# A two-layer graph kernel: five blocks of layer 0 one step later, the last rows' x in a tile of its own, and the next pair turned inside the current pair's products

## The chip, the cores and the metric

The kernel runs on one core of one Trainium2 chip. The metric is the device time of one execution in microseconds (us). The time before is the median of 13 runs, 1067.2 us. The core's engines work at the same time, each through its own queue in order: PE (TensorE, matrix products, with PEld for its weight loads), DVE (VectorE), ACT (ScalarE), POOL (GpSimd, here mostly indirect DMAs that gather or scatter rows) and SP (SyncE, which issues plain DMAs).

## The reference

`x` has 2708 rows of 1024 numbers, `adj` is a sparse 2708 x 2708 matrix of zeros and ones, and everything is float32.

```python
# layer 0
q = x @ W_q.T + b_q;  k = x @ W_k.T + b_k;  v = x @ W_v.T + b_v
z = (q @ k.T) / sqrt(1024) * adj
attn = softmax(where(z == 0, -10000, z), axis=1)
x = layernorm(x + relu(attn @ v))
# layer 1
x = layernorm(x + adj @ (x @ weight) + bias)
```

## The kernel before

**Sparse form.** The kernel lists the few neighbours of each row and sorts the rows by their number. The sorted rows form 22 blocks of 128; block `b` has `SLOTS[b]` neighbours for each row (block 0 has 15, blocks 18 to 20 have one, block 21 holds rows without neighbours). A block's part in layer 0 is: gather a row of `y` for each of its rows and the `x` rows of its neighbours (POOL, line 349), score them (DVE, line 813), softmax, add up the weighted neighbours into a tile `r` (DVE, line 870), turn `r` with 8 PE transposes per row block (line 716) and an ACT copy out of PSUM (line 717), and multiply by `W_v` ("project"). The 32 busiest rows, the "hub", are dealt over the whole tile and joined with block 0 (lines 947 to 967).

**The y stage.** `y` is x times a product of the key and query weights. `y_block(b)` runs 16 matmuls of 128x512 for 128 rows of x (line 319), two DVE adds out of PSUM into the tile `yo` (line 323), 8 column sums on ACT (line 332), the load of a later block's transposed x into one of three tiles `xt`, and a store of `yo`. Block 21 holds only 20 rows of x and goes another way (line 305). After it `xbT`, the mean of x, is ready, which the blocks with few neighbours need.

**The list of steps in layer 0.** `steps` is written out by hand. ("y", b) is a block of the y stage. ("v", b) projects one block alone (line 739); it is followed, at the next step, by `finish0`, whose two DVE bias adds (line 906) take the products out of PSUM. ("p", pair) projects two blocks at once. Before each step `run_job` is called as long as a written credit lasts; each call gathers and scores a piece of one block. Jobs in `late_jobs` start when the y stage is over. The names `got`, `turned` and `done0` keep which blocks are added up, turned and done. At most three tiles `r` (`RB`) are held at a time.

**Pairs.** For two blocks the product with a 1024x1024 matrix is taken in seven half products instead of eight (one level of Winograd's scheme). `turn_pair` turns both blocks and forms four sums `S` of the turned halves on DVE (lines 988 to 991) in one buffer, `s_all`. `differences` are three or four differences of weight quarters. `pair_products` issues the seven half products, each 4 matmuls of 128x512 (line 999), into PSUM banks `pa`, `pb`, `pc`, with DVE adds between them (line 1011). Its first two products, `a11 * w11` and `a12 * w21`, need only the turned block, the others need `S` or the second block. Layer 1 works the same way in `units` of one or two blocks: `sum_rows` adds up gathered rows of layer 0's output (line 1241), `gather_x1` prepares x plus bias (line 1251 and a gather), `turn1` turns, `work1` multiplies, `finish1` normalizes and scatters. The adds marked `URGENT` go ahead in DVE's order.

**What sets the order.** The order in which the Python code issues instructions, with a scheduler's priorities, sets each engine's queue. So where the code issues a turning decides what stands in front of it on PE, and whatever stands behind a DVE or POOL instruction that waits, waits too.

Of the kernel before, what the change touches and what calls it, by code (L numbers as in the profile page):

```python
# [80 lines left out]
def sparse_part(ctx, tc, x, xT, adj, wqT, wkT, wvT, bq, bk, bv, w1, b1, out):  # L81
# [29 lines left out]
    with es:  # L111
# [158 lines left out]
        xts = []  # L270

        def load_x():
            b = len(xts)
            if b == NB:
                return
            r0, n = b * P, rows[b]
            xt = xa.tile([P, DC, P], F32, name="xt", bufs=3)
            if n < P:
                nc.gpsimd.memset(xt, 0.0)
            nc.sync.dma_start(out=xt[:, :, :n], in_=xT[:, r0:r0 + n].rearrange("(c p) n -> p c n", p=P))  # L280
            xts.append(xt)
# [48 lines left out]
        def column_sums(b, behind=None):  # L330
            for c in range(DC):
                put = nc.scalar.activation(junka, xts[b][:, c, :], AF.Copy, accum_out=xs[:, c, b:b + 1])  # L332
                if behind is not None and c % 2 == 0:
                    follow(put, behind[c // 2])
# [642 lines left out]
        def turn_pair(flips, pool):  # L977

            A = []
            for k, flip_to in enumerate(flips):  # L980
                rT = (pool if k else wp).tile([P, DC, P], F32, name="rT", bufs=2)
                A.append(flip_to(rT))
            if len(flips) == 1:
                return A, None
            (a11, a12), (a21, a22) = [(a[:, :DC // 2], a[:, DC // 2:]) for a in A]
# [5 lines left out]
            halves_turned.append(nc.vector.tensor_sub(S[3], a12, S[1]))  # L991
            return A, S

# [18 lines left out]

        def pair_products(A, S, w, ts, base, to, whole, first_alone=False):

# [8 lines left out]
            half_products(pb, a12, w21)  # L1023
            whole(0, 0, pb, to[0][0])
            if first_alone:
                half_products(pc, S[0], t1, stop=False)
# [25 lines left out]

        def project_pair(pair, A, S):
# [6 lines left out]
            pair_products(A, S, wv_q, wv_t, [bias, bias], [halves_of(t) for t in ts], whole, pair == pairs[-1])  # L1060
            return ts

        def finish_pair(pair, ts):
            for k, (b, t) in enumerate(zip(pair, ts)):
# [9 lines left out]
                else:  # L1074
# [13 lines left out]
        jobs, late_jobs = jobs + late_jobs, len(late_jobs)  # L1088
        steps = [("y", 8), ("y", 9), ("y", 10), ("y", 11), ("y", 12), ("v", 6), ("y", 13), ("v", 5), ("y", 14), ("v", 4), ("y", 15), ("v", 3),
                 ("y", 16), ("v", 2), ("y", 17), ("y", 18), ("y", 19), ("y", 20), ("y", 21)]  # L1090
        steps += [("v", b) for b in [1, 0] + last] + [("p", pair) for pair in pairs]
# [16 lines left out]
        def turn0(b):  # L1108
# [4 lines left out]
            return flip_shares([got["hub"], got[0]]) if b == 0 else flip(got[b])  # L1113

        credit = -STEP
        turned, done0 = {}, set(last)
        pending = None
        left_y = NB - FAMILY
        for i, (kind, b) in enumerate(steps):
# [29 lines left out]
            for k, c in steps[i:i + 2]:  # L1149
                if k != "y" and c not in turned and not (left_y and k == "p"):  # L1150
                    turned[c] = turn0(c) if k == "v" else turn_pair([lambda rT, r=got[b_]: flip(r, rT) for b_ in c], xb_pools[0])
                    done0.update(blocks_of((k, c)))
            if kind == "y":
# [11 lines left out]
            elif kind == "v":  # L1165
                xr = gather_x(x, b)
                pending = finish0, b, (project_mean if b in last else project)(turned[b], wv_q), xr
            else:
                for b_ in b:
                    pair_x[b_] = gather_x(x, b_)  # L1170
                pending = finish_pair, b, project_pair(b, *turned[b])
        w1_q = quarters_of("w1")
# [97 lines left out]

        def work1(unit, A, S, xrs):

# [13 lines left out]
            if S is None:  # L1286
                (a11, a12), x0 = halves_of_turned(A[0]), xs_[0]
                pa, pb = bank(), bank()
                half_products(pa, a11, w11, stop=False)
                add(x0[1], pa, x0[1])  # L1290
                half_products(pb, a11, t1, stop=False)
                half_products(pb, a12, w22, start=False)
# [3 lines left out]
            else:  # L1296
                pair_products(A, S, w1_q, w1_t, xs_, xs_, whole, unit == units[-1])
            return ts, sums
# [3 lines left out]
        got1[1] = [sum_rows(b, k) for k, b in enumerate(units[1])]  # L1302
        turned1[0] = turn1(units[0], got1.pop(0))
        follow(nc.vector.tensor_sub(t1, t1, w11), firsts[0], same=True)
        nc.vector.tensor_sub(t2, w22, t1)
# [3 lines left out]
        for i, unit in enumerate(units):  # L1309
            for p in pending:  # L1310
                finish1(*p)
            if i + 1 < len(units):
                turned1[i + 1] = turn1(units[i + 1], got1.pop(i + 1))
                xrs[i + 1] = [gather_x1(b, k) for k, b in enumerate(units[i + 1])]
            if i == 0:
                got1[2] = [sum_rows(b, k, halves_turned[-1]) for k, b in enumerate(units[2])]
            if i + 3 < len(units):
                got1[i + 3] = [sum_rows(b, k) for k, b in enumerate(units[i + 3])]
            if i == 4:
                sum_rows("hub")  # L1320
            pending = list(zip(unit, *work1(unit, *turned1.pop(i), xrs.pop(i))))
            if i == 2:
# [321 lines left out]
```

## Time and profile before

| what | value |
|---|---|
| median of 13 runs | 1067.2 us |
| lowest and highest run | 1065.22 and 1073.03 us |
| the profiled execution | 1066.3 us |
| its span in the trace | 1064.6 us (1.7 us lie around it) |
| PE busy | 1004.9 us |
| DVE busy | 849.8 us |
| POOL busy | 493.9 us |
| ACT busy | 425.5 us |

The table's busy times are from the page of the profiled execution, and overlap. Places in the trace are given in us from the start of the span. By these the y stage of the second family of blocks runs to about 523, the single projections to about 559, the pairs of layer 0 from 563 to 747, and layer 1 from 758 on. A wait in the profile is named by the line that waited and the line that released it. A name such as `r` stands for all its buffers.

### The profile page before, as it was taken

How to read it: one execution, taken by the hardware profiler on the slowest of the kernel's cores; microseconds unless marked ns; L12 is line 12 of the kernel's file. 1: busy time of each engine (PE TensorE's matmuls, PEld its weight loads, DVE VectorE, ACT ScalarE, POOL GpSimd, SP SyncE). 2: the span in 40 equal slices, each digit the busy share in tenths (PEclk: the TensorE clock that was granted, in tenths of full speed). 3: DMA queues.
4: the chain of work that ended last, by engine and by line, in shares of the span. 5: the costliest groups of instructions: out<-in, count | busy, mean ns of one | idle time of the engine just before them, and what ended most of it. 6: DMA issues, size and time to landing. Idle time of an engine off the chain costs nothing.

```text
span 1064.6 us, 10216 instructions
## 1 busy us (share of the span) xinstructions
PE 1004.9 (94%) x2849; PEld 473.6 (44%) x2849; DVE 849.8 (80%) x1831; ACT 425.5 (40%) x894; POOL 493.9 (46%) x397
## 2 busy tenths in 40 slices
PE   7999999999989999999999999999589999999993
PEld 6444444444443444444545444444234444454441
DVE  8799999995287889999399999965678877896532
ACT  4688788422042332224424344332323363333321
POOL 1000140057654546526157666511677777887300
PEclk9999999999999999999999999999799999999997
DMA  9555458565887656796442777726689599979701
GB/s 358 190 206 202 165 209 292 159 214 171 293 249 254 206 192 201 227 342 192 171 124 88 246 240 264 265 80 217 154 296 262 186 286 311 289 212 321 194 40 42
DMA packets 90963, 229.20 MB, mean 215 GB/s; under 512 B 18411, under 2 KB 40395, under 8 KB 88189
## 3 DMA queue, kind: packets, MB, share of 16 engines
q0 software_dynamic: 48768, 148.05, 44.0%
q1 hardware_dynamic: 42128, 80.41, 22.0%
q8 instruction: 24, 0.39, 0.2%
q14 instruction: 43, 0.34, 0.1%
HBM read 219.61 MB, written 33.68 MB: 238 GB/s over the span
## 4 chain that ended last, share of the span: by engine, by line
PE 19%; DVE 16%; issue 7%; DMA 5%; ACT 2%; POOL 1%; POOLq 0%; DVEq 0%; ACTq 0%
PE po L999 17%; DVE r L1241 3%; DVE r L870 3%; DMA g<-x_d,tabs 2%; DVE junkv L813 2%; PE po L739 1%; DVE t L1011 1%; DMA yg<-y_d,tabs 1%; PE tr L716 1%; DVE part L1241 1%; ACT junks L775 1%; DMA g<-x_d,tab 1%; PE tr L729 1%; DVE t L1069 1%; POOL g L349 1%
## 5 line engine op out<-in xcount | busy, mean ns | idle before, releaser
L319 PE MATMUL po<-m_sb,xt 128*128 128x512 f32 x672 | 292.3, 593 | 4.1 <-DVE yo L323 4.1
L319 PEld LDWEIGHTS po<-m_sb,xt 128*128 128x128 f32 x672 | 126.4, 190 | 160.5 <-issue 151.4
L813 DVE SCALAR_TENSOR_TENSOR junkv<-yg,g 128x1024 uint8<-128x1024 f32 x109 | 132.9, 1219 | 32.5 <-DMA g<-in_x_dram,tabs 14.7
L349 POOL DMA_INDIRECT g<-in_x_dram,tabs x86 | 110.8, 1288 | 71.5 <-DVE r L870 20.8
L999 PE MATMUL po<-t,s_all 128*128 128x512 f32 x272 | 123.0, 594 | 2.4 <-DVE xr L1011 2.4
L1241 DVE SCALAR_TENSOR_TENSOR r<-g,valid,r 128x1024 f32<-128x1024 f32 x77 | 98.5, 1281 | 21.6 <-DMA g<-x_d,tabs 21.0
L609 PE MATMUL po<-wk_o,wq_o 128*128 128x512 f32 x256 | 110.5, 592 | 0.0
L739 PE MATMUL po<-wv,rT 128*128 128x512 f32 x224 | 97.8, 593 | 2.5 <-DVE pr L855 1.9
L775 ACT ACTIVATE junks<-t,lnm 128x1024 uint8<-128x1024 f32 (+1 forms) x41 | 47.0, 1146 | 126.7 <-DVE lnm L773 97.2
L349 POOL DMA_INDIRECT g<-x_d,tabs x67 | 77.5, 1156 | 22.7 <-issue 13.7
L563 POOL DMA_INDIRECT tab_d<-rec,pos_i x22 | 27.1, 1230 | 130.0 <-DVE pos_i L552 123.6
L999 PE MATMUL po<-w,rT 128*128 128x512 f32 x192 | 86.4, 599 | 0.0
L870 DVE SCALAR_TENSOR_TENSOR r<-g,pr,r 128x1024 f32<-128x1024 f32 x64 | 81.7, 1278 | 5.9 <-ACT r L882 4.6
L332 ACT ACTIVATE junka<-xt 128x128 f32<-128x128 f32 x176 | 53.8, 306 | 74.4 <-PE po L319 56.7
L788 ACT ACTIVATE t<-t,nmr,rstd 128x1024 f32<-128x1024 f32 (+1 forms) x41 | 50.0, 1237 | 79.7 <-DVE nmr L787 78.6
L999 PEld LDWEIGHTS po<-t,s_all 128*128 128x128 f32 x272 | 51.1, 190 | 68.1 <-issue 59.1
L224 DVE MAX8 few<-a 128x8 f32<-128x75 f32 (+3 forms) x132 | 79.2, 618 | 0.0
L609 PEld LDWEIGHTS po<-wk_o,wq_o 128*128 128x128 f32 x256 | 48.3, 190 | 59.3 <-issue 59.1
L999 PE MATMUL po<-w,s_all 128*128 128x512 f32 x160 | 72.1, 592 | 0.0
L221 DVE SCALAR_TENSOR_TENSOR a<-a,iota 128x2708 f32<-128x2708 f32 (+1 forms) x22 | 65.2, 2963 | 5.4 <-ACT junk L220 5.4
L739 PEld LDWEIGHTS po<-wv,rT 128*128 128x128 f32 x224 | 42.2, 190 | 55.4 <-issue 54.3
L717 ACT COPY rT<-tr 128x512 f32<-128x512 f32 x80 | 43.0, 586 | 52.5 <-PE tr L716 52.5
(350 smaller groups left out, 1523.8 us busy)
## 6 DMA issues: line engine op xcount, KB each, us to landing
a<-in_adj_dram SPq DMA_DIRECT2D x21, 1354.0 KB, 5.8
xt<-in_xT_dram SPq DMA_DIRECT2D x21, 512.0 KB, 5.0
y_d<-yo SPq DMA_DIRECT2D x21, 512.0 KB, 5.9
g<-in_x_dram SPq DMA_DIRECT2D x21, 512.0 KB, 7.8
wq_i<-in_wqT_dram SPq DMA_DIRECT2D x8, 512.0 KB, 9.0
wk_i<-in_wkT_dram SPq DMA_DIRECT2D x8, 512.0 KB, 10.2
wv<-in_wvT_dram SPq DMA_DIRECT2D x16, 256.0 KB, 6.1
w<-in_w_dram SPq DMA_DIRECT2D x4, 1024.0 KB, 7.6
```

The source lines that it names most:

```text
L221: nc.vector.scalar_tensor_tensor(a[:n], a[:n], 1.0, iota[:n], op0=ALU.is_equal, op1=ALU.mult)
L224: nc.vector.max(few[:n, i * 8:(i + 1) * 8], a[:n, cuts[i]:cuts[i + 1]])
L319: put = nc.tensor.matmul(po, xt[:, c, :], m_sb[c // 2][:, c % 2, k0:k1], start=(c == 0), stop=(c == DC - 1))
L332: put = nc.scalar.activation(junka, xts[b][:, c, :], AF.Copy, accum_out=xs[:, c, b:b + 1])
L349: nc.gpsimd.indirect_dma_start(out=dst[:n], out_offset=None, in_=src, in_offset=bass.IndirectOffsetOnAxis(ap=at, axis=0), bounds_check=N - ...
L609: nc.tensor.matmul(po, wq_o[i // 2][:, o, i % 2 * P:(i % 2 + 1) * P], wk_o[:, o, hs], start=(o == 0), stop=(o == DC - 1))
L739: put = nc.tensor.matmul(acc, rT[:, c, :], w[c // 4][h][:, c % 4, :], start=(c == 0), stop=(c == DC - 1))
L775: nc.scalar.activation(junks[:n], t[:n], AF.Square, bias=nm[:n], accum_out=vs[:n])
L813: nc.vector.scalar_tensor_tensor(junkv[:n], yg[:n, :D], scale, xg[:n], op0=ALU.mult, op1=ALU.mult, accum_out=s)
L870: nc.vector.scalar_tensor_tensor(r[:n], xg[j][:n], pr[:n, j:j + 1], r[:n], op0=ALU.mult, op1=ALU.add)
L999: put = nc.tensor.matmul(acc, a[:, k], w[:, k], start=start and k == 0, stop=stop and k == DC // 2 - 1, skip_group_check=True)
L1241: put = nc.vector.scalar_tensor_tensor(r[:n], xg[:n], ok[:n, j:j + 1], r[:n], op0=ALU.mult, op1=ALU.add)
```

## The change

Three things are changed. First, in `steps` the projections of blocks 6, 5, 4, 3 and 2 each stand one y block later. Second, x of block 21 gets a tile of its own, `xt_last`, 128 x 8 x 32, which DVE clears and SP loads ahead of all other tiles of x; its column sums read 32 columns instead of 128. Third, `turn_pair` no longer forms the sums: `pair_sums` does, after the products of the pair before. The turning of the next pair is handed to `pair_products` as `between` and issued behind the first two half products of the current pair. In layer 1 units 2 and 3 are now gathered behind the products of unit 0, and later units in the same turn as before.

```diff
+        xt_last = xa.tile([P, DC, HUB], F32, name="xt_last", bufs=1)
+        nc.vector.memset(xt_last, 0.0)
+        nc.sync.dma_start(out=xt_last[:, :, :rows[-1]], in_=xT[:, (NB - 1) * P:].rearrange("(c p) n -> p c n", p=P))
         def load_x():
...
+            if b == NB - 1:
+                xts.append(xt_last)
+                return
             xt = xa.tile([P, DC, P], F32, name="xt", bufs=3)
-            if n < P:
-                nc.gpsimd.memset(xt, 0.0)
...
-                put = nc.scalar.activation(junka, xts[b][:, c, :], AF.Copy, accum_out=xs[:, c, b:b + 1])
+                put = nc.scalar.activation(junka[:, :xts[b].shape[2]], xts[b][:, c, :], AF.Copy, accum_out=xs[:, c, b:b + 1])
...
-            if len(flips) == 1:
-                return A, None
+            return A
+
+        def pair_sums(A):
+            if len(A) == 1:
+                return None
             (a11, a12), (a21, a22) = [(a[:, :DC // 2], a[:, DC // 2:]) for a in A]
...
-            return A, S
+            return S
...
-        def pair_products(A, S, w, ts, base, to, whole, first_alone=False):
+        def pair_products(A, S, w, ts, base, to, whole, between, first_alone=False):
...
             half_products(pb, a12, w21)
             whole(0, 0, pb, to[0][0])
+            between()
...
-        steps = [("y", 8), ("y", 9), ("y", 10), ("y", 11), ("y", 12), ("v", 6), ("y", 13), ("v", 5), ("y", 14), ("v", 4), ("y", 15), ("v", 3),
-                 ("y", 16), ("v", 2), ("y", 17), ("y", 18), ("y", 19), ("y", 20), ("y", 21)]
+        steps = [("y", 8), ("y", 9), ("y", 10), ("y", 11), ("y", 12), ("y", 13), ("v", 6), ("y", 14), ("v", 5), ("y", 15), ("v", 4), ("y", 16),
+                 ("v", 3), ("y", 17), ("v", 2), ("y", 18), ("y", 19), ("y", 20), ("y", 21)]
...
+        def turned_pair(pair):
+            done0.update(pair)
+            return turn_pair([lambda rT, r=got[b_]: flip(r, rT) for b_ in pair], xb_pools[0])
+
+        sums0 = {}
...
-                if k != "y" and c not in turned and not (left_y and k == "p"):
-                    turned[c] = turn0(c) if k == "v" else turn_pair([lambda rT, r=got[b_]: flip(r, rT) for b_ in c], xb_pools[0])
-                    done0.update(blocks_of((k, c)))
+                if k == "v" and c not in turned:
+                    turned[c] = turn0(c)
+                    done0.add(c)
+            if kind == "v" and steps[i + 1][0] == "p":
+                turned[pairs[0]] = turned_pair(pairs[0])
+                sums0[pairs[0]] = pair_sums(turned[pairs[0]])
...
-                pending = finish_pair, b, project_pair(b, *turned[b])
+                following = steps[i + 1][1] if i + 1 < len(steps) else None
+                pending = finish_pair, b, project_pair(b, turned[b], sums0[b], lambda: turned.update(
+                    {following: turned_pair(following)} if following else {}))
+                if following:
+                    sums0[following] = pair_sums(turned[following])
...
                 half_products(pa, a11, w11, stop=False)
                 add(x0[1], pa, x0[1])
+                between()
...
             if i + 1 < len(units):
-                turned1[i + 1] = turn1(units[i + 1], got1.pop(i + 1))
                 xrs[i + 1] = [gather_x1(b, k) for k, b in enumerate(units[i + 1])]
-            if i == 0:
-                got1[2] = [sum_rows(b, k, halves_turned[-1]) for k, b in enumerate(units[2])]
-            if i + 3 < len(units):
+            if 0 < i < len(units) - 3:
                 got1[i + 3] = [sum_rows(b, k) for k, b in enumerate(units[i + 3])]
             if i == 4:
                 sum_rows("hub")
-            pending = list(zip(unit, *work1(unit, *turned1.pop(i), xrs.pop(i))))
+            pending = list(zip(unit, *work1(unit, turned1.pop(i), sums1.pop(i), xrs.pop(i), lambda: turned1.update(
+                {i + 1: turn1(units[i + 1], got1.pop(i + 1))} if i + 1 < len(units) else {}))))
+            if i + 1 < len(units):
+                sums1[i + 1] = pair_sums(turned1[i + 1])
+            if i == 0:
+                for u in (2, 3):
+                    got1[u] = [sum_rows(b, k, halves_turned[-1]) for k, b in enumerate(units[u])]
```

More of the change, by code (lines that the diff above doesn't have):

```diff
@@ L1051, in halves_of_turned, with project_pair @@
             return a[:, :DC // 2], a[:, DC // 2:]
-        def project_pair(pair, A, S):
+        def project_pair(pair, A, S, between):
             ts = [(xb_pools[0] if k else wp).tile([P, D], F32, name="t", bufs=2 + k) for k in range(2)]
@@ L1058, in whole @@
                 add(halves_of(ts[k])[h], acc, what)
-            pair_products(A, S, wv_q, wv_t, [bias, bias], [halves_of(t) for t in ts], whole, pair == pairs[-1])
+            pair_products(A, S, wv_q, wv_t, [bias, bias], [halves_of(t) for t in ts], whole, between, pair == pairs[-1])
             return ts
@@ L1269, in turn1, with work1 @@
                               for b, r in zip(unit, rs)], cp)
-        def work1(unit, A, S, xrs):
+        def work1(unit, A, S, xrs, between):
             ts = [wp.tile([P, D], F32, name="t", tag="t" if k % 2 == 0 else "yg") for k, _ in enumerate(unit)]
@@ L1296, in work1 @@
             else:
-                pair_products(A, S, w1_q, w1_t, xs_, xs_, whole, unit == units[-1])
+                pair_products(A, S, w1_q, w1_t, xs_, xs_, whole, between, unit == units[-1])
             return ts, sums
@@ L1303, in sparse_part @@
         turned1[0] = turn1(units[0], got1.pop(0))
+        sums1 = {0: pair_sums(turned1[0])}
         follow(nc.vector.tensor_sub(t1, t1, w11), firsts[0], same=True)
```

## The prediction, made before the changed kernel was run

> **What bounds the kernel now.** I read the page's busy times first: PE is busy 1004.9 of 1064.6 us. The change removes no PE product, so it can gain only where PE stands still. The second view is therefore the list of who waited for whom, PE's lines.
>
> ```profile
> PE tr L716 <- DVE r L1238: 11.7, 1, 11.7
> PE po L319 <- DVE yo L323: 4.1, 5, 1.3
> ...
> PE tr L716 <- ACT rT L717: 3.1, 2, 2.4
> PE tr L716 <- DVE r L870: 2.9, 4, 1.3
> ...
> PE po L999 <- DVE xr L1011: 2.4, 4, 1.4
> PE tr L716 <- DVE r L1241: 2.1, 1, 2.1
> PE po L739 <- DVE pr L855: 1.9, 1, 1.9
> ...
> PE tr L729 <- DVE r L1241: 0.8, 1, 0.8
> PE po L305 <- DMA xt<-in_xT_dram: 0.4, 1, 0.4
> ```
>
> The columns are the total, the number and the longest wait in us. The change of layers (11.7) is untouched. What the change can reach are the waits at the turning (`tr L716`, `tr L729`), of the products for their adds (`L999`), and of block 21 for its x (`L305`). The third view is PE's timeline at the last pairs of layer 0; square brackets give the idle time ahead of a row and who ended it.
>
> ```profile
> 691.30 3.60 PE L999 MATMUL po<-t,rT 128*128 128x512 f32 x8
> 695.35 1.07 PE L716 MATMUL tr<-ident,r 128*128 128x128 f32 x8 [0.45 <-DVE nms L840]
> 696.25 3.60 PE L999 MATMUL po<-wv,rT 128*128 128x512 f32 x8
> 701.12 1.06 PE L716 MATMUL tr<-ident,r 128*128 128x128 f32 x8 [1.27 <-DVE r L870]
> 702.02 3.60 PE L999 MATMUL po<-wv,rT 128*128 128x512 f32 x8
> 705.46 3.60 PE L999 MATMUL po<-t,s_all 128*128 128x512 f32 x8
> ```
>
> Blocks 13 and 12, the last pair, are turned before and inside the first products of pair (9, 14). Each half product holds PE 3.44 us (705.46 - 702.02), the turning of a block 0.90. PE stood still 1.27 us for r of block 12, and 2.25 us in five places from 623.8 on (0.20, 0.16, 1.23, 0.21, 0.45): 3.52 in all. The fourth view, the chain of what ended last, says what follows:
>
> ```profile
> 699.70 1.29 DVE r L870
> 701.12 1.06 PE tr L716 x8
> 702.18 44.65 PE po L999 x104
> ```
>
> From 702 to 747 nothing but PE sets the time; before that the chain runs over DVE, busy 57.57 of 60 us from 640 to 700. So layer 0 ends at "r of block 12 is ready", plus its turning, plus the products issued behind it.
>
> **The turning inside the products, layer 0.** `between` puts the turning of 13 and 12 behind both first half products of (9, 14) instead of before and between them. PE work stays the same; one half product more stands ahead of the wait for block 12. PE comes free at 694.90 now, 1.80 earlier (693.10) without the four earlier waits; two half products, 6.87, end at 699.97; block 13 is turned by 700.9-701.0. r of 12 is ready at 699.70 + 1.28 = 700.98; the present row starts 0.14 later, so its turning ends at 702.02 and `S1*t2` starts there instead of at 705.46. That is 3.44 us less, minus d, by which DVE reaches r of 12 later. The four sums are issued after the current pair's products, but `s_all` has one buffer, so they could not run sooner before; until `S1*t2` of the next pair two half products and two turnings (8.7 us) hide four sums of 0.68 each. If that cover went, they would cost 2.7.
>
> **The steps and d.** Block y13 (13.9 us) now runs ahead of v6, so v6's second half ends at about 362.3. In DVE's order the two L906 adds of v6 kept their place: their second part ran at 354.70 and must now wait till 362.3, 7.6 us. Behind it stand L908, the scores and adds of the following jobs, and on POOL the gathers that need their `g` tiles. PE does not wait at once, since free banks take the next products. The wait repeats for no later block, because DVE then is late itself. What takes it up is DVE's idle time around block 21: 5.16 + 1.76 + 4.41 = 11.33 us between 507.5 and 521.5. Block 0's last adds (L947) end at 504.7 now; with what idle there is before them they come to about 508.5, at the most 512.5. The mean `xbT`, now ready at 524.74, then stands between 524.3 and 526.7. I take d = 0.4 (-0.4 to 2): the rows' idle time exceeds the delay by 3.7. SP's constants for blocks 8 on go two y stores earlier; SP waits only for these stores, and the three `xt` tiles cover it. The 1.92 wait at 332.6 for a bank that a yo add frees stays.
>
> **x of the last rows.** The own tile removes the 0.38 wait (`po L305 <- DMA xt`), POOL's clearing of the tile (0.96) and three quarters of each of 8 column sums. The clearing on DVE, a quarter as wide, falls before 300, where PE has its own work; bounds 0 and 0.96, I take 0 on the path. As r of block 12 sets layer 0's end, the 0.38 belongs to d and is not added again. Layer 0: 3.44 - 0.4 = 3.0 less (1.4 to 3.9).
>
> **Layer 1.** The 2.10 wait at 779.3 goes, but the next are DVE's: the two adds L1011 of unit (19, 18) stand behind L1241 adds that wait for POOL's gathers, in the new order as in the old. The first comes about 0.8 sooner; the second still stands behind the same eleven L1241 and ends at about 798.2, which PE meets at 798.36: 0.15 gained. At 843.5 0.1 of 0.2. At 864.9 PE waits 2.44 for the copy L717. In ACT's new order copies of bias (L1251, held to 864.34 by a scatter), L775 and L788 still stand before that copy, which ends at about 871.3, while two half products later PE wants it at about 869: I take 0.6 (0.4 to 2.44). At 954.3 block 0's L1241 gets 6.9 us more: 0.7 of 0.79. Sum 1.55 (0.4 to 3.5). New waits for units 2 and 3, whose gathers moved behind unit 0, I bound by what such waits cost here, 0 and 1.4 (the longest L1011 wait); 0 is taken since POOL's order before them is nearly unchanged. Tail unchanged.
>
> **A rule on the clock.** The windows:
>
> ```profile
> 750.00:764.00 14.00, 5.17 (x18) 3.40 (x18) 5.29 (x9) 7.34 (x10) 8.20 (x6) 0.53 0.48 144
> 764.00:800.00 36.00, 31.52 (x90) 14.92 (x91) 29.26 (x35) 7.24 (x13) 28.87 (x22) 1.00 0.87 263
> 860.00:870.00 10.00, 7.57 (x31) 4.06 (x30) 5.23 (x15) 6.84 (x14) 7.87 (x8) 1.00 0.96 312
> ```
>
> The column before the last two is PE's granted clock. After the 11.67 wait it was 0.53 over 14 us, while after waits of 2.10 and 2.44 it stayed 1.00. So the removed waits give their own widths and no clock. The slow stretch cost about 2.6 us (turnings and products near 1.9 instead of 1.0).
>
> The Trainium skill ("TensorE: Matmul & The Clock Gate", Part 1) says that an idle window of about 3.4 us halves the clock and 3.4 us of work restores it. It too gives no gain for 2.44; after a long wait it would charge 1.7, less than this trace's 2.6, and its recovery is far shorter than the 14 us here.
>
> **Sum.** 3.0 + 1.55 = 4.55 less. The profiled execution takes 1066.3 (span 1064.6 + 1.7), so 1061.75 for its like; it lies 0.9 under the median 1067.2. On the median: 1062.6.
>
> **Rivals.** *All reachable waits go*: layer 0 3.9, layer 1 0.5 + 2.44 + 0.79, 7.6 less, 1059.6. For it: none of these waits belongs to work that is always late. Against: ACT's order at 865 and POOL's pace at 798.
>
> *DVE or POOL keeps its pace*: d between 2.5 and 6, or as much lost in new waits of layer 1, for DVE is 96% busy before 700. Then 1065.1 to 1068.6; I name 1066.5. Against it: the chain itself shows r of block 12 reached one half product too early.
>
> *Slower*: DVE's wait at L906 of v6 isn't taken up, because POOL's gathers start late too and each job keeps the distance. Its whole 7.6 goes into d, block 0 is turned late (L729 at 525.9), and everything DVE does till 701 with it: -3.44 + 7.6 - 1.55 = +2.6, 1069.8, and up to 1072.4 if PE's wait there is long enough for the slow clock's 2.6. It decides from d = 7.1 on (3.44 + 1.55 + 2.1). For it: DVE had only 0.64 idle at 353 and 3.02 at 361.5. Against: 11.33 idle at 507.5. That the turning does not move is excluded by PE's order.
>
> **How the numbers follow.** Forecast (1060.5 to 1065) 0.5, all waits 0.1, pace 0.14, slower 0.26. A measurement tells 0.2%, 2.1 us, from no change: 0.60 faster, 0.14 same, 0.26 slower. The range reaches from 1059.3, just under the best case, to 1070.3, past the slower rival's first price; what lies outside is its clock part and sums of new waits.
>
> **What would show it.** Right: PE's row of turnings at 701 moves behind the second half product, and no wait over 0.3 remains from 620 to 705; DVE idle at L906 near 355 for about 7 us, and less than 5 at 507 to 521; block 0 turned at 525 to 528; `L305 <- DMA xt` gone; the 2.10 at 779 gone, but a wait for L1011 just before 798 of 1.5 to 2. Wrong: r of block 12 later than 703, a wait over 2 for L729 near 525, or layer 1 (from 758 on in the present trace) longer than now.

## The result, and the profile after

The changed kernel took 1080.08 us (median of 7 runs, 1077.19 to 1083.28) beside 1067.55 us for the kernel before on the same chip: a ratio of 1.0116 with a 95% interval of 1.0096 to 1.0135, some 12.4 us longer. The forecast was 1062.6 and its range ended at 1070.3: wrong in sign and in size. The profiled execution took 1076.58 us, span 1074.5; it is none of the seven and a little quicker than each of them, so the two traces can account for 9.9 us of span. In the new kernel the lines below 280 keep their numbers and the later ones move: L721, L722 turn and copy (L716, L717 before), L1007 and L1019 multiply and add (L999, L1011), L960 turns `nm` (L955), L734 turns block 0 (L729), L324 and L328 are the y products and adds, L780 the squares (L775).

PE's list of waits after the change (total, number, longest, in us):

```profile
PE tr L721 <- DVE r L1260: 11.7, 1, 11.7
PE tr L721 <- ACT rT L722: 10.7, 7, 3.7
PE po L324 <- DVE yo L328: 6.3, 5, 2.0
PE tr L960 <- DVE nm L939: 5.2, 1, 5.2
...
PE po L1007 <- DVE xr L1019: 3.3, 2, 3.0
...
PE po L744 <- ACT rT L722: 0.7, 1, 0.7
PE tr L734 <- DVE r L1263: 0.6, 1, 0.6
```

The waits that the change aimed at are gone: `r` of layer 0 (2.9 before), `r` of layer 1 (2.1), and `xt` (0.4). Three others stand in their place: the copies of the turned rows (3.1 before, 10.7 now), a wait for `nm` that was not there at all, and longer waits for the y adds.

**By stage**, from PE's timeline of the two profiles:

| stage | before | after | difference |
|---|---|---|---|
| to the first y product | 140.9 | 142.0 | +1.1 |
| y stage to block 21 | 370.7 | 376.2 | +5.5 |
| block 21 to the turning of block 0 | 14.1 | 13.6 | -0.5 |
| from there to the first turning of layer 1 | 232.9 | 231.2 | -1.7 |
| layer 1 to PE's end | 288.8 | 294.7 | +5.9 |
| tail | 17.2 | 16.8 | -0.4 |

Nothing ties the first row to the change. PE waits 2.2 us for `hot` near 122 us in both traces, and the 38 products behind that wait ran slower in the trace after. PE before the change, then after it:

```profile
122.58 0.50 PE L539 MATMUL mm<-hot,lower 128*128 128x152 f32 x2 [2.23 <-DVE hot L533]
...
123.17 16.47 PE L609 MATMUL po<-wk_o,wq_o 128*128 128x512 f32 x38
```

```profile
121.92 0.50 PE L544 MATMUL mm<-hot,lower 128*128 128x152 f32 x2 [2.21 <-DVE hot L538]
...
122.52 18.17 PE L614 MATMUL po<-wk_o,wq_o 128*128 128x512 f32 x38
```

The granted clock from 122 to 126 us was 1.00 before and 0.63 after. Two kernels of the experiments that have no part of the change in common show the same (0.58 over 4 us with the steps alone, 0.57 with the late units alone), and the own tile alone does not (1.00).

**The y stage.** DVE after the change, at the bias adds of block 6 (L911, L906 before) and at `nm` of block 0:

```profile
357.18 0.68 DVE L911 TENSOR_TENSOR t<-po,bias_bc 128x512 f32<-128x512 f32 x1
362.24 0.69 DVE L911 TENSOR_TENSOR t<-po,bias_bc 128x512 f32<-128x512 f32 x1 [4.38 <-PE po L744]
...
508.08 0.15 DVE L939 TENSOR_TENSOR nm<-nm 128x1 f32<-128x1 f32 x1
```

The stand at L911 is as predicted in place and end (362.24, foretold 362.3); it shows as 4.38 and not 7.6 because DVE reached the first add 3.1 late already. DVE and PE before the change, at `nm` and its transpose:

```profile
496.25 0.15 DVE L934 TENSOR_TENSOR nm<-nm 128x1 f32<-128x1 f32 x1
...
503.18 0.30 PE L955 MATMUL tr<-ident,nm 128*128 128x128 f32 x1
```

and after it:

```profile
508.38 0.45 PE L960 MATMUL tr<-ident,nm 128*128 128x128 f32 x1 [5.23 <-DVE nm L939]
508.62 9.66 PE L324 MATMUL po<-m_sb,xt 128*128 128x512 f32 x18
```

Before, `nm` was ready at 496.40 and PE wanted it at 503.18: a slack of 6.8. After, it came at 508.2, 11.8 later. The transpose stands in PE's queue ahead of the rest of a y block, so PE stood. The 18 matmuls behind it took 9.66, where 18 at the same place took 7.89 before: the granted clock was 0.53 in the 4 us after the wait. The 11.8 can be followed on DVE between 340 us and `nm`: it stood 12.1 us for gathered rows before and 19.3 after, which is 7.2 more, and 4.4 at L911.

**Layer 0's last pairs**, PE after the change:

```profile
699.70 7.03 PE L1007 MATMUL po<-wv,rT 128*128 128x512 f32 x16
706.56 1.47 PE L721 MATMUL tr<-ident,r 128*128 128x128 f32 x12
707.87 1.02 PE L1007 MATMUL po<-t,s_all 128*128 128x512 f32 x2
710.22 0.66 PE L721 MATMUL tr<-ident,r 128*128 128x128 f32 x4 [1.32 <-ACT rT L722]
```

Twelve of the 16 transposes of blocks 13 and 12 now run without a wait for `r`; the last four wait 1.32 for a copy.

**Layer 1**, PE after the change, in unit (17, 16):

```profile
821.37 1.47 PE L721 MATMUL tr<-ident,r 128*128 128x128 f32 x12
826.53 1.11 PE L721 MATMUL tr<-ident,r 128*128 128x128 f32 x4 [3.68 <-ACT rT L722]
827.43 4.68 PE L1007 MATMUL po<-t,s_all 128*128 128x512 f32 x8
```

and ACT at the same time:

```profile
819.28 1.05 ACT L1273 COPY xr<-bias 128x1024 f32<-128x1024 f32 x1 [6.23 <-DVE t L1300]
824.20 1.15 ACT L780 ACTIVATE junks<-t,lnm 128x1024 uint8<-128x1024 f32 x1 [3.87 <-DVE lnm L778]
...
825.90 1.54 ACT L722 COPY rT<-tr 128x512 f32<-128x512 f32 x3
```

ACT before the change, at the same turning:

```profile
809.40 2.05 ACT L717 COPY rT<-tr 128x512 f32<-128x512 f32 x4 [2.09 <-PE tr L716]
811.31 1.08 ACT L1251 COPY xr<-bias 128x1024 f32<-128x1024 f32 x1
813.71 1.15 ACT L775 ACTIVATE junks<-t,lnm 128x1024 uint8<-128x1024 f32 x1 [1.32 <-DVE lnm L773]
```

Before, the turning came ahead of the squares of the unit before, and its copies met a free ACT. Two half products later it now meets the squares, which stand in ACT's queue and wait for DVE's mean (`lnm`); the copies wait behind them, and PE's last transposes for the copies. This unit took 31.2 us in place of 25.8: 3.68 of the 5.4 is the wait, and the slow clock behind it explains about the rest.

### The profile page after: what moved, and what is told of

Same layout as the page of the kernel before. It is cut to its first block, busy times and chain, and to the rows that moved or that the text cites. A ratio compares the mean times of both kernels' runs of the same rounds, so it can differ in the third digit from the quotient of the medians.

```text
span 1074.5 us, 10211 instructions
## 1 busy us (share of the span) xinstructions
PE 1008.2 (94%) x2849; PEld 475.5 (44%) x2849; DVE 851.0 (79%) x1832; ACT 424.7 (40%) x894; POOL 498.0 (46%) x396
## 5 line engine op out<-in xcount | busy, mean ns | idle before, releaser
L324 PE MATMUL po<-m_sb,xt 128*128 128x512 f32 x672 | 294.1, 596 | 6.3 <-DVE yo L328 6.3
L324 PEld LDWEIGHTS po<-m_sb,xt 128*128 128x128 f32 x672 | 127.1, 191 | 163.9 <-issue 152.7
L818 DVE SCALAR_TENSOR_TENSOR junkv<-yg,g 128x1024 uint8<-128x1024 f32 x109 | 132.8, 1218 | 38.6 <-DMA g<-in_x_dram,tabs 18.4
L354 POOL DMA_INDIRECT g<-in_x_dram,tabs x86 | 115.4, 1342 | 73.7 <-DVE r L875 23.4
L1007 PE MATMUL po<-t,s_all 128*128 128x512 f32 x272 | 124.5, 598 | 3.3 <-DVE xr L1019 3.3
L1263 DVE SCALAR_TENSOR_TENSOR r<-g,valid,r 128x1024 f32<-128x1024 f32 x77 | 98.6, 1281 | 19.0 <-DMA g<-x_d,tabs 18.3
L780 ACT ACTIVATE junks<-t,lnm 128x1024 uint8<-128x1024 f32 (+1 forms) x41 | 47.0, 1146 | 119.1 <-DVE lnm L778 97.4
L354 POOL DMA_INDIRECT g<-x_d,tabs x67 | 81.2, 1213 | 22.7 <-issue 15.2
L1007 PE MATMUL po<-w,rT 128*128 128x512 f32 x192 | 86.3, 602 | 0.0
L337 ACT ACTIVATE junka<-xt 128x128 f32<-128x128 f32 x168 | 51.4, 306 | 81.2 <-PE po L324 65.0
L1007 PEld LDWEIGHTS po<-t,s_all 128*128 128x128 f32 x272 | 50.5, 192 | 60.3 <-issue 54.5
L1007 PE MATMUL po<-w,s_all 128*128 128x512 f32 x160 | 72.4, 593 | 0.0
L722 ACT COPY rT<-tr 128x512 f32<-128x512 f32 x80 | 42.7, 584 | 56.0 <-PE tr L721 56.0
```

The costliest lines, as they stand in the source:

```text
L324: put = nc.tensor.matmul(po, xt[:, c, :], m_sb[c // 2][:, c % 2, k0:k1], start=(c == 0), stop=(c == DC - 1))
L337: put = nc.scalar.activation(junka[:, :xts[b].shape[2]], xts[b][:, c, :], AF.Copy, accum_out=xs[:, c, b:b + 1])
L354: nc.gpsimd.indirect_dma_start(out=dst[:n], out_offset=None, in_=src, in_offset=bass.IndirectOffsetOnAxis(ap=at, axis=0), bounds_check=N - ...
L818: nc.vector.scalar_tensor_tensor(junkv[:n], yg[:n, :D], scale, xg[:n], op0=ALU.mult, op1=ALU.mult, accum_out=s)
L1007: put = nc.tensor.matmul(acc, a[:, k], w[:, k], start=start and k == 0, stop=stop and k == DC // 2 - 1, skip_group_check=True)
L1263: put = nc.vector.scalar_tensor_tensor(r[:n], xg[:n], ok[:n, j:j + 1], r[:n], op0=ALU.mult, op1=ALU.add)
```

## The experiments

Ratios are to the kernel before on the same chip, with 95% intervals. In experiments 2, 5, 6, 8 (second kernel) and in the squares of 4 the kernel before took 1067.4 to 1067.8 us, in the others 1078 to 1079, where no profile of the kernel before was taken. The profiles of the latter show 7 to 10 us of waits named "issue" in the y products (`po L319`, 260 to 282), those of the former none; so a y stage is compared within its group, and traces by the length of a stage. The quoted expectations carry the theories' names of their time; what follows each says the finding by content.

**1. The parts alone.** Each takes one part of the diff and leaves the others as before.

> Only the list of steps is the changed one; x of block 21, the turning in layer 0 and layer 1 are as before. Theory A+B (two separate losses: A the steps, which make DVE late until PE waits for nm of block 0 at L960, and B the turning in layer 1, whose ACT copies stand behind the norm's work): layer 0 ends 6 to 8 us later, layer 1 is as long as before, 1073 to 1075.5 us, with a PE wait of about 5 us for nm near 503. Rival R1 (the steps are the whole loss; layer 1 only suffers from their lateness): 1077 to 1081. Rival R2 (the turning is the whole loss): 1066 to 1069, no wait for nm.

> Only the turning in layer 0 is moved inside the products; steps, x of block 21 and layer 1 are as before. Theory A+B: the waits for r between 620 and 702 go, a wait for the copy of rT of up to 1.5 us may come near 705, layer 0 ends 1.5 to 3.4 us sooner: 1064 to 1066. Rival R1: the same. Rival R2: ACT's copies cost as much as they bring, 1067 to 1070.

> Only layer 1 is the changed one; layer 0 is as before. Theory A+B: PE waits some 10 us in all for copies of rT and 3 for the add L1011 in layer 1, which is 5 to 8 us longer: 1072.5 to 1075.5. Rival R1: layer 1 alone gains, 1065 to 1067. Rival R2: 1076 to 1080.

> Only x of block 21 has its own tile; all else is as before. All theories: the wait of 0.38 us for its load goes, 0 to 0.5 us less, 1067 to 1067.6, which can't be told from no change.

| part | ratio | what moved (us) |
|---|---|---|
| list of steps | 1.0029 (1.0002 to 1.0056) | the wait for `nm` |
| turning inside, layer 0 | 1.0004 (0.9980 to 1.0028) | block 0's turning to layer 1: 232.8, waits 3.9 (before 232.9, 3.5) |
| turning inside, layer 1 | 1.0062 (1.0041 to 1.0082) | layer 1: 298.5 (before 288.8 and 287.8 in two profiles) |
| own tile for the last rows | 0.9993 (0.9965 to 1.0022) | wait for `xt` gone; block 21 to block 0: 13.4 (14.1) |

PE in the kernel with the steps alone, and in that with layer 0's turning alone:

```profile
521.60 0.29 PE L955 MATMUL tr<-ident,nm 128*128 128x128 f32 x1 [4.44 <-DVE nm L934]
```

```profile
661.47 0.66 PE L716 MATMUL tr<-ident,r 128*128 128x128 f32 x4 [1.40 <-ACT lv L778]
...
716.58 0.66 PE L716 MATMUL tr<-ident,r 128*128 128x128 f32 x4 [1.32 <-ACT rT L717]
```

The profile of the steps alone is of an execution 9.8 us longer than that kernel's median (1091.54 beside 1081.78). Its layer 1 (296.0) has a wait of 6.8 us for an add and one of 12 us on POOL at a scatter, so it shows where `nm` waits but not what the list costs. The profile of layer 1's turning alone is also the longest of its six runs (1089.08, median 1086.30), so 298.5 is on the high side. Two parts cost and two do nothing that can be measured. The sum, 0.29 + 0.04 + 0.62 - 0.07 = 0.88%, lies just under the whole change's interval (0.96 to 1.35), but with the intervals of the four parts it is uncertain by about 0.5, so no gap between parts and whole is shown.

**2. The change with the old list of steps.**

> The whole change but the list of steps, which is that of before. If the parts add up: 12.5 us of loss less the steps' 3 to 6, so 6 to 9 us more than before, all of it in layer 1. If the steps are the whole loss: no more than before. If the turning is the whole loss: 11 to 13 more.

Measured 1.0063 (1.0042 to 1.0084); y stage 370.2, layer 1 296.3. So inside the change the list costs 1.16 - 0.63 = 0.53%, some 5.6 us, and the rest is what the layer-1 part costs alone.

**3. Copies first.** In each turning the copies go ahead of the earlier unit's norm work on ACT. The edit in layer 1 (layer 0: `finish_pair` in the same way; the third kernel has both, the own tile and the old steps):

```diff
-            for p in pending:
-                finish1(*p)
-            if i + 1 < len(units):
-                xrs[i + 1] = [gather_x1(b, k) for k, b in enumerate(units[i + 1])]
...
+            def between(i=i, pending=pending):
+                if i + 1 < len(units):
+                    turned1[i + 1] = turn1(units[i + 1], got1.pop(i + 1))
+                    ahead[:] = [copies[-1]] if 0 not in units[i + 1] else []
+                for p in pending:
+                    finish1(*p)
+                if i + 1 < len(units):
+                    xrs[i + 1] = [gather_x1(b, k) for k, b in enumerate(units[i + 1])]
...
```

The squares and the bias copies follow the copy in `ahead` on ACT. The gathers of later units move behind the turning with them.

> Layer 0 as before; layer 1 turns the next unit inside the products, but the finishing of the unit before, its bias copies and the next sums are issued behind the turning, and ACT's squares and bias copies are ordered behind the four copies of rT. Differences are from the kernel before on the same chip. Theory B (layer 1 loses because the copies of rT stand in ACT's queue behind work that waits): the waits for rT go and the loss of 6.7 us with them, to between 3 less and 1 more. Rival (the loss is the place of the turning itself, or units 2 and 3 being gathered later): 4 to 7 more, as with the turning alone, and waits for the adds L1011 remain.

> Layer 1 as before; layer 0 turns the next pair inside the products, and the finishing of the pair before is issued behind that turning, its squares ordered behind the copies of rT. Theory B for layer 0 (waits for r were replaced by waits for copies of rT, 3.9 us for 3.5): 2 to 3.4 us less than before, no wait over 0.5 us between 620 and 720. Rival (r of the last blocks, or DVE, sets the time anyway): within 1 us of before.

> The old list of steps, x of block 21 in its own tile, and both layers turned inside the products with the copies of rT first. If theories A and B hold and add up: 2 to 6 us less than before. If the turning inside the products brings nothing: within 1.5 us of before. If it loses even so: 3 or more us more.

Measured 1.0061 (1.0037 to 1.0086), 1.0025 (0.9998 to 1.0052) and 1.0077 (1.0049 to 1.0106): no gain at all. PE's waits in the first of them:

```profile
PE po L1006 <- DVE xr L1018: 6.0, 7, 1.7
PE po L1006 <- DVE r L1259: 5.1, 1, 5.1
```

The waits for copies went (11.0 with the turning alone); as much came for DVE's adds (11.1 in these two lines). The edit also makes the norm later: the first scatter of layer 1 starts 47.5 us after the layer's start, 38.6 with the turning alone. So it shows that removing the copies' wait in this way gains nothing, not that the wait is free.

**4. Only the squares behind the copies**, in layer 1 (`follow(put, copies[-1], same=True)` for each square, no other line moved).

> Layer 1 turned inside the products as in the change (layer 0 as before), and ACT's squares of the norms ordered behind the copies of rT of the same unit; nothing else is moved by hand. Theory E: the waits for copies behind squares go, 5 to 8 us less than with the turning alone, within 1.5 us of before or less. Rival F: 4 to 7 us more than before, as waits for L1011's adds.

Measured 1.0057 (1.0038 to 1.0077). The same picture: 1.7 left for copies, 7.5 for DVE's adds, and the first scatter again later, at 43.8 us of the layer.

```profile
PE po L1004 <- DVE xr L1016: 7.5, 7, 2.3
...
PE tr L718 <- ACT rT L719: 1.7, 1, 1.7
```

**5. One turning put back.** Layer 1 as changed, but the turning of the unit after (17, 16) stands before its products as in the kernel before (`if i == 2: turned1[3] = turn1(...)` ahead of `work1`).

> Layer 1 as in the change (layer 0 as before), except that unit (15, 1) alone is turned ahead of the products of unit (17, 16), as in the kernel before; POOL's order is the same as with the turning alone. Theory E (the loss of layer 1 is nearly all one wait: the copies of rT for (15, 1) stand in ACT's queue behind a square that waits for the norm of the unit before, 3.7 to 5.4 us, and the slow clock after it): that wait goes, the unit ends 25.8 us after the one before, layer 1 is 5 to 7 us shorter than with the turning alone: 0 to 2.5 us more than before. Rival F (DVE and POOL set the pace of layer 1, the wait only shows it): the time comes back as waits for adds or later turnings, still 4 to 7 more.

Measured 1.0052 (1.0028 to 1.0075). The wait for the copy at this place is gone, and PE stands as long for an add:

```profile
824.57 5.40 PE L1002 MATMUL po<-t,s_all 128*128 128x512 f32 x8 [4.37 <-DVE xr L1014]
```

Ahead of that add DVE had stood 5.84 us for a gather (0.63 at the same sum before the change): the gathers were late already. Here nothing was pushed behind the copies, so at this place the copy is where PE stands and not the cause of the length.

**6. The scatters of layer 1 later in POOL's queue**, in the kernel before and with the layer-1 change (`scatter(out, ...)` is kept in a list and issued behind a later unit's gathers).

> The kernel before, but in layer 1 the scatter of a finished unit is issued behind the gathers of a later unit, so that POOL's queue does not stand still for a norm while gathers stand behind it. Theory C (layer 1 is paced by POOL's queue, and its end is the last gather plus some 66 us of products): POOL's 4.6 us of waiting at scatters before the last gather mostly go, layer 1 is 2.5 to 4.5 us shorter, 2 to 5 us less than before. Rival D (the gathers' own length sets the pace, or PE's order): within 1.5 us of before.

> Layer 1 turned inside the products as in the change, layer 0 as before, and the scatters of layer 1 issued behind gathers of a later unit. Theory C: POOL's 7.8 us of waiting at scatters go, layer 1 is 5 to 8 us shorter than with the turning alone: between 1 less and 2 more than before. Rival D: still 4 to 7 more than before, the last gather still 6 us later than in the kernel before.

Measured 1.0070 (1.0048 to 1.0091) and 1.0101 (1.0076 to 1.0126). The remedy costs more than the illness, and so says little: in the kernel before, POOL's waits for scatters fell from 4.7 to 0.1 us and its last gather came 7.0 to 8.5 us sooner in the layer (215.6 after its start, 224.1 and 222.6 in two profiles without the edit), but the turning of block 0 then stood in PE's queue ahead of products that ran without a wait behind it:

```profile
948.53 0.74 PE L729 MATMUL tr<-to,r 128*128 128x96 f32 x2 [7.36 <-DVE r L1255]
```

**7. Which turnings cost.** Layer 1 alone, the turnings of the first three units as before and the later ones inside (`inside(i)` is `i > 2`), or the other way round (`i <= 2`); the third kernel is the candidate, with the own tile and late units only.

> Layer 1 alone; the first three turnings stand before the pair's products as before the change, all later ones inside. Theory H (the loss begins at the first turnings: the norm of unit (20) on ACT falls behind the copies of the first unit's turning, POOL's scatter of it waits some 1.5 us more, the gathers after it come 2 to 5 us later and the lateness is never made up): second unit's pitch near 26 us as before, last gather of layer 1 some 222 to 226 us after its start, layer 1 from its start to PE's end 286 to 291, time within 2 us of before. Rival (each turning inside its pair's products costs its bit, the first ones no more than the others): 2 to 5 us longer than before, last gather 226 to 230.

> Layer 1 alone; only the first three turnings stand inside the pair's products, all later ones before them as before the change. Theory H: unit (17,16) has a pitch of 31 us or more, last gather 229 to 233, layer 1 294 to 300, time 5 to 9 us above before, about the whole of what the layer-1 change cost by itself (6.6). Rival (each turning costs its bit): 1 to 4 us above before, and the pitch of the second unit under 29.

> Old list of steps, own tile for the last rows of x, layer 0 as before, layer 1 turned inside from the fourth unit on: the candidate. Theory H: as the run with late units alone, less the 0.4 us of the wait for x of block 0, so 0 to 3 us below before. Rival: 2 to 5 us above before.

| kernel | ratio | layer 1 (us) | last gather after layer 1's start |
|---|---|---|---|
| before, two profiles | | 288.8, 287.8 | 224.1, 222.6 |
| late units inside | 1.0019 (0.9993 to 1.0044) | 292.3 | 226.1 |
| first units inside | 1.0064 (1.0036 to 1.0091) | 295.6 | 229.1 |
| candidate | 1.0007 (0.9986 to 1.0029) | 292.1 | 225.9 |
| all inside (1.) | 1.0062 (1.0041 to 1.0082) | 298.5 | 231.5 |

The first three turnings alone cost what all of them cost (0.64 of 0.62%), with unit (17, 16) 31 us long. The late ones cost 0.19% with an interval that holds nothing; their trace is 3.5 to 4.5 us longer, more than theory H gave them and within its rival's numbers, and again the first turning inside waits for copies. PE with the first units inside, then with the late ones:

```profile
803.26 0.65 PE L716 MATMUL tr<-ident,r 128*128 128x128 f32 x4 [3.54 <-ACT rT L717]
804.70 6.62 PE L1002 MATMUL po<-t,s_all 128*128 128x512 f32 x8 [0.79 <-DVE xr L1014]
```

```profile
886.41 0.66 PE L716 MATMUL tr<-ident,r 128*128 128x128 f32 x4 [4.24 <-ACT rT L717]
886.90 5.29 PE L1002 MATMUL po<-t,s_all 128*128 128x512 f32 x8
```

What the first turnings do to POOL shows at the scatter of unit (20). POOL before the change:

```profile
794.81 1.14 POOL L703 DMA_INDIRECT out_dram<-t,tabs  x1 [0.76 <-ACT t L788]
```

and with layer 1's change alone, where layer 1 begins 12.6 us later:

```profile
809.89 1.85 POOL L703 DMA_INDIRECT out_dram<-t,tabs  x1 [2.28 <-ACT t L788]
```

The scatter starts 2.4 us later in the layer and ends 3.1 later, and all gathers of the units to come stand behind it. The four copies of the next turning now stand ahead of the last step of that unit's norm on ACT, but this step does not wait for them. ACT before the change, with layer 1's change alone, and in the changed kernel:

```profile
793.29 1.24 ACT L788 ACTIVATE t<-t,nmr,rstd 128x1024 f32<-128x1024 f32 x1 [4.70 <-DVE nmr L787]
```

```profile
808.38 1.24 ACT L788 ACTIVATE t<-t,nmr,rstd 128x1024 f32<-128x1024 f32 x1 [5.45 <-DVE nmr L787]
```

```profile
800.44 1.24 ACT L793 ACTIVATE t<-t,nmr,rstd 128x1024 f32<-128x1024 f32 x1 [6.07 <-DVE nmr L792]
```

In all three ACT stands idle until DVE has `nmr`. From the mean to `nmr` DVE took 8.2 us before, with five sums of gathered rows and one add in between; it took 9.9 and 10.6 in the other two, with six sums and two adds. The mean itself came 0.7 and 0.4 later in the layer. So what delays this scatter is DVE's queue. In the changed kernel the scatter starts at 38.96 of the layer, 2.8 later than before, and waits only 0.95, because the gathers ahead of it took longer (18.3 us for the last 14 of them, 16.1 before). With layer 1's change alone POOL has no slack to win this back: from there to its last gather it works through its queue with 0.30 between instructions, but for two more such waits. In every kernel but the two of experiment 6, layer 1 ends 64 to 68 us after the last gather, so a later last gather goes with a longer layer. In the two of experiment 6 it is 80 and 76.

One rival is not taken apart by a run: the kernels with the first turnings inside also gather units 2 and 3 behind the products of unit 0. In the traces POOL's first 54 gathers and scatters of layer 1 are of the same kinds in the same order before the change, after it and in the kernels of the table, so this move does not show in POOL's queue; in DVE's it may.

No version beat the kernel before. For five of them (the own tile, layer 0's turning with and without copies first, the late units, the candidate) the interval holds no change.

**8. The steps: is it the stand at L906, or the joining of block 0?** First, block 0 joined one y block later, so that `nm` has more time; second, the bias adds of blocks 6 to 2 behind the next y block's adds, so that DVE does not stand.

```diff
-                if i >= entry[1] + 2:
+                if i >= (entry[1] + 2 if entry[0] != 0 else 18 if entry[1] < 18 else 19):
```

```diff
-                pending[0](*pending[1:])
+                if kind == "y" and pending[0] is finish0:
+                    held = pending
+                else:
+                    pending[0](*pending[1:])
...
                 y_block(b)
+                if held:
+                    held[0](*held[1:])
```

In the second kernel the adds of these blocks are also ordered behind the y adds on DVE.

> Only the steps are changed as in the change, and the joining of block 0 with the hub is issued one y block later (its transpose of nm before block 21, its rest before the next step). Theory A (the steps cost what PE waits for nm, ahead of y blocks that were ready): the 4 to 5 us wait at the transpose of nm goes; 0 to 1.5 us more than before instead of 3.1. Rival (DVE's lateness itself sets the end of layer 0, wherever PE waits): the wait moves to the turning of block 0 or to the pairs' r, 3 to 4 us more than before.

> The steps of the change alone, but the bias adds of blocks 6 to 2 stand in DVE's queue behind the adds of the next y block, so that DVE does not stand still for v6. Theory A2 (the wait of 4.4 us at these adds, kept to the end of the y stage, makes nm late): DVE's idle time at L906 near 362 goes, PE's wait for nm shrinks from 4 to 5 to below 1 us, and the time is within 1.5 us of before. Rival G (DVE is late for other reasons: gathers that come later, row constants that moved ahead of block 0): the wait for nm stays above 3 us, 2 to 6 us more than before.

Measured 1.0056 (1.0029 to 1.0083) and 1.0035 (1.0016 to 1.0054). In neither does PE wait for `nm`, which confirms where it stood in the change; neither is faster than the steps alone (1.0029). With the join moved, block 0 comes late at the next place (block 21 to its turning 20.5 instead of 14.1). With the adds held back the y stage is still 378.3 beside 370.7 and 372.8 before (371.8 and 373.5 in two kernels with the old list on the same chip), by other waits:

```profile
PE po L319 <- DVE yo L323: 8.6, 6, 2.2
```

This points to DVE's lateness, and not to the one wait for `nm`, as what the new list buys. It is not shown outright: each variant moves other work too, and the profile of the late join is of an execution 10 us above its median (1095.18 beside 1085.08).

**9. The kernel before once more**, for the size of chance in a trace.

> The kernel before itself, for its profile on the chip of the experiments: all theories expect the stages of the other kernels there, y stage near 382 us, from the turning of block 0 to layer 1 near 233, layer 1 near 289.

Span 1065.3; y stage 372.8 (370.7; not the 382 expected, as this chip is one of those at 1067 us), layer 1 287.8 (288.8), last gather 222.6 (224.1). Stage lengths of these two profiles of one kernel differ by 1 to 2 us; the 5 to 10 us above are more than that.

## Why the prediction was wrong, step by step

**The turning inside the products, layer 0: -3.44.** PE's row did move behind the second half product, and its wait for `r` went, as foretold. But the term measured 0.1 alone and 1.7 within the change. The step that failed is "PE comes free ... 1.80 earlier without the four earlier waits": it took `r` for the only thing a turning waits for. A turning needs ACT's copies too, and once moved it met ACT at its squares. 3.5 us of waits became 3.9 in the kernel with this part alone, 2.0 in the change.

**The steps and d: 0.4 (at most 2).** Measured 5.5 in the y stage, and 0.29% alone, 0.53% within the change. Three readings failed. "PE does not wait at once" looked to L729 at 525 as the first transpose that could miss its input; the transpose of `nm` stands at 503 with 6.8 us of slack, and DVE was 11.8 late there. The delay was taken as the 7.6 of one stand; the stand was 4.4, and DVE's waits for gathered rows grew by 7.2 on the way to `nm`, as the slower rival said. And the 11.33 us of idle DVE at 507 came too late to help a transpose at 503; 6.57 of it is still there at 525. Block 0 was turned at 531.78, outside the 525 to 528 of the forecast. In the two kernels of experiment 8 the wait for `nm` is gone and the time is not better, so repairing the first reading alone would not have given the time.

**x of the last rows: 0.** Right: the wait went, the time did not move.

**Layer 1: -1.55.** Measured +5.9, 0.62% alone: the largest miss. Single old waits were read well: the 2.10 at 779 went (2.57 for a copy at 792.96 came), L1011's next add was met late at 804.10 (4.4 us of it is the later start of the layer), block 0's 0.79 became 0.63. The step that failed is the bound for "new waits for units 2 and 3 ... 0 and 1.4", with 0 taken because POOL's order is nearly unchanged. The order was (the first 54 gathers and scatters are the same); the times were not. DVE's order, which decides when a norm and its scatter are ready, was taken from the trace before. ACT's order was looked up at 865 alone, where an old wait stood, not at the turnings of the first units, where none did. The sum lists old waits and strikes them out; it has no line for what a turning now meets.

**The clock.** The prediction read 0.53 over 14 us as the recovery after a long wait, and priced new waits at their width. Finer windows of the trace after show that most of that stretch was the idle time itself. Columns as before; the third from the end is the granted clock:

```profile
759.00:763.00 4.00, 0.00 (x0) 0.03 (x1) 0.89 (x2) 1.99 (x2) 2.46 (x3) 0.50 0.07 19
763.00:767.00 4.00, 4.00 (x11) 2.71 (x12) 3.07 (x2) 1.17 (x2) 3.39 (x3) 0.50 0.79 241
767.00:771.00 4.00, 4.00 (x16) 2.06 (x15) 3.23 (x3) 0.38 (x1) 3.70 (x2) 0.85 0.96 159
```

Recovery takes some 5 us of work here, much nearer to the 3.4 us of the Trainium skill ("TensorE: Matmul & The Clock Gate", Part 1) than the prediction claimed against it. And new waits can cost the clock:

```profile
804.10:808.10 4.00, 4.00 (x10) 1.84 (x11) 3.29 (x4) 0.00 (x0) 3.39 (x3) 1.00 0.82 168
...
826.53:830.53 4.00, 4.00 (x9) 2.28 (x10) 3.95 (x9) 3.14 (x7) 3.39 (x3) 0.61 0.96 171
```

After 3.01 us of waiting the clock stayed full, after 3.68 it was 0.61 for 4 us. The prediction's "no clock" for waits of 2.10 and 2.44 holds for the execution it was read from only: in the second profile of the kernel before, waits of 2.07, 2.23 and 2.97 us were followed by 0.67, 0.65 and 0.57.

**The rivals.** "All waits go" was furthest off. "DVE or POOL keeps its pace" named the thing that decides layer 1, with "as much lost in new waits of layer 1", but bounded it by the gain, at 1068.6. Its prices are also 0.4 too high as a sum, since its d is added to a forecast that already holds d = 0.4. "Slower" had the right mechanism for the list (the stand is not taken up, gathers start late too), and the wrong place; with 0.26 it was held too low. No case let two parts lose together, and the range ended with the first price of one.

**What stays open.** That the layer-1 loss begins in the kernels that turn the first units inside is shown, and that taking away the copies' wait in three ways gained nothing. How the lateness divides between the scatter's wait, POOL's gathers (1.21 us each in the change and 1.18 to 1.19 in two profiles of before, for 109 of them) and DVE's sums is not: moving the scatters disturbed too much else. In the changed kernel the waits at scatters before the last gather grew only from 4.7 to 5.3 us, and the gathers took some 3 us more in all. Why DVE runs one sum and one add more ahead of the first norm is not shown either.

## What to carry to other kernels

When a step is moved later on the busiest engine, look up what each of its helpers on the other engines is doing at the new place, the copies out of PSUM and the sums that norms and gathers wait for: a wait that is struck out of the list says nothing of the ones to be met. Take the slack of every instruction in the bound engine's queue behind the moved work, not only of those that wait today; the first with less slack than the delay is where it shows. And where a queue runs almost without gaps, as POOL's gathers here, do not count on it to win back a delay of 2 us early on, whichever wait it is booked under.

## What the runs showed of the hardware

The same short wait on PE can cost the clock or leave it. Near 122 us PE waits 2.2 us for `hot` in all 20 traces. In 16 of them the granted clock over the next 4 us was 1.00; in four (the change, the change with the old list, the steps alone, the late units alone) it was 0.57 to 0.64. Before the change, then after it:

```profile
122.00:126.00 4.00, 3.42 (x11) 1.95 (x12) 4.00 (x13) 1.55 (x3) 0.00 (x0) 1.00 0.72 301
```

```profile
122.00:126.00 4.00, 4.00 (x9) 1.94 (x10) 4.00 (x9) 0.82 (x2) 0.00 (x0) 0.63 0.59 246
```

Other waits of 2 to 3.5 us went both ways too: after 2.57, 3.01 and 3.47 us the next 4 us ran at full clock, after 2.07, 2.23, 2.97, 3.29 and 3.36 us at 0.57 to 0.67. All 16 waits of 3.5 us or more behind earlier work, the change of layers apart, were followed by 0.50 to 0.65. So below 3.5 us the width alone does not tell; what does, no run here shows.

Where the clock fell, the price can be read: eight matmuls that take 3.60 took 5.3 to 5.4 after 3.29, 3.36, 4.24 and 4.37 us (4.68 after 3.68, with the transposes ahead of them 0.45 longer; 6.62 after 3.54, where a second wait followed). So such a wait cost some 1.5 to 1.8 us more than its width.
